# Two halves of the TensorE array for the products of a two-layer graph kernel

## The chip, the cores and the metric

The kernel runs on one core of a Trainium2 chip. The metric is device time in microseconds. Before the change it takes 2409.18 us, the median of three runs (2409.16 to 2414.54).

## The reference

There are 16 graphs (batches) of 1024 nodes with 128 features, each with a dense 1024 x 1024 adjacency matrix of zeros and ones. Two layers follow each other, each with a residual sum and a normalisation over the features:

```python
# layer 0
h = x @ Ww.T + Wb
e = (h @ A) @ h.T;  e = e + e.T
attention = softmax(where(adj > 0, e, 0), axis=1) * adj
hp = relu(attention @ h)
ic, fc, oc = three gates: sigmoid(hp @ wi_u + x @ wi_x), ...
x = layernorm(x + oc * tanh(ic * hp + fc * x))
# layer 1, with four heads
h = x @ conv_w[hd] + conv_b[hd]
scores = (h @ attn_w[hd]) @ h.T
hh = relu(tanh(adj * scores) @ h)
x = layernorm(x + relu(relu(mean of hh over the heads) + x))
```

Everything is in fp32. The largest parts of the work are, for each batch, the four 1024 x 1024 score matrices of layer 1 (a product over 128 features) and the four products of their tanh with h (a product over 1024 nodes).

## The kernel before

A product on TensorE has a stationary operand (128 rows by up to 128 columns, loaded into the array) and a moving operand, of which up to 512 columns stream past it; the result lands in a bank of PSUM, with the stationary columns as partitions. Everywhere in this kernel the contraction uses 128 rows, and in nearly all products the stationary operand has 128 columns.

Layer 1 is the larger part. For each batch there are 4 heads times 8 blocks of 128 nodes, 32 steps. `layer1_step` (line 687) of one step issues two score products (line 704), one for each half of 512 moving columns, into two PSUM tiles of the pool `ps_sc`, which has four of them. VectorE (DVE) multiplies each with the adjacency (line 705), ScalarE applies tanh to the 1024 columns (line 706), and `back` (line 708) multiplies the result with h of this block and head, accumulating over the 8 blocks into `acc`, two banks of PSUM (line 710). `back` isn't issued at once: `push` (line 194) holds it back for two steps. After a head's last block `add_head` (line 722) takes relu of the accumulator and adds it to a sum over heads; the next head reuses the same two banks.

Before the steps of a batch, `rows` (line 670) computes h of all four heads for each block (line 675), and `head_uT` with `project_T` (line 234, product in line 238) computes uT of a head, the operand of its scores.

Layer 0 of the next batches is woven into these steps. Its pieces have short names: Q is qT (`project_T`), H is h (`multiply_h`, line 335), S the scores (line 354), T their transposition through DVE and memory, A mask and exponentials, B the weighing with attention (`back` in line 455, product in line 462). The dictionaries `BETWEEN`, `AHEAD` and `FIRST` say after which step which piece is issued. This order is written by hand and each engine executes its own instructions in the order of the program; a framework inserts the waits between engines. Batch 0's layer 0 and the last head of the last batch have an order of their own, in which transpositions go through TensorE.

Of the kernel before, what the change touches and what calls it, by code (L numbers as in the profile page):

```python
# [19 lines left out]
P = 128  # L20
# [4 lines left out]
def two_layer_adjacency_kernel(  # L25
# [19 lines left out]
    nc = tc.nc  # L45
    B, N, D = x.shape
    H = conv_w.shape[0]
    assert D == P and N % 512 == 0
    NB = N // P
    NH = N // 512  # L50
# [10 lines left out]
    def small(name):  # L61
        return ps_sc.tile([P, 512], F32, tag="sc", name=name)
# [23 lines left out]
    wwT_g = consts.tile([P, G], F32, name="wwT_g")  # L86
# [39 lines left out]
    q_w = consts.tile([P, P], F32, name="q_w")  # L126
    c_col = wwT_g[:, G - 1 : G]
# [6 lines left out]
    def keep_at_work(n):  # L134
        for _ in range(n):
            nc.tensor.matmul(idle[:, :P], warm[:, :P], warm[:, :P], start=True, stop=True)  # L136

    keep_at_work(6)
    pa, pw, ps, pc = small("p_a"), small("p_ww"), small("p_s"), small("p_c")
    nc.tensor.transpose(pa[:, :P], a_in, ident)  # L140
# [53 lines left out]
    def push(back):  # L194
        pending.append(back)
        if len(pending) > DELAY:
            pending.popleft()()
# [33 lines left out]
                ALU.subtract, ALU.mult,  # L231
            )

    def project_T(dst, w, src, bias, name, halves=range(NH)):

        for q in halves:
            ps = small(f"pT_{name}_{q}")
            nc.tensor.matmul(ps, w, src[:, ts(q, 512)], start=True, stop=True)  # L238
            if bias is None:
                nc.scalar.copy(dst[:, ts(q, 512)], ps)  # L240
            else:
                nc.scalar.activation(dst[:, ts(q, 512)], ps, AF.Identity, bias=bias)
# [44 lines left out]
    def layer0(b):  # L287
# [3 lines left out]


        t = {}

        def load_xT():
            t["xT"] = sb.tile([P, N], F32, tag="xT", name=f"xT_{b}")
            nc.sync.dma_start(t["xT"], xT[b])
# [10 lines left out]
        def project_q(q):  # L308
            if q == 0:
                t["qT"] = sb.tile([P, N], F32, tag="qT0", name=f"qT0_{b}", bufs=1)  # L310
            if (b, q) == (0, 1):
                ps = small("pT_q0_second")
                nc.tensor.matmul(ps, q_w, t["xT"][:, 512:], start=True, stop=True)
                nc.vector.tensor_scalar_add(t["qT"][:, 512:], ps, c_col)
                return
            if (b, q) != (0, 0):
                return project_T(t["qT"], q_w, t["xT"], c_col, f"q0_{b}", [q])
            t["pq"] = small("pT_q0_first")
            nc.tensor.matmul(t["pq"], q_w, t["xT"][:, :512], start=True, stop=True)

# [6 lines left out]
        def multiply_h(g):  # L327

            if g == 0:
                t["h"] = sb.tile([P, NB, G], F32, tag="h0", name=f"h0_{b}", bufs=1)  # L330
            ks = GROUPS[g]
            ps = small(f"pR_h0_{b}_{g}")[:, : len(ks) * G]
            t["ph", g] = ps = ps.rearrange("p (k d) -> p k d", d=G)
            for i, k in enumerate(ks):
                nc.tensor.matmul(ps[:, i, :], t["xT"][:, ts(k, P)], wwT_g, start=True, stop=True)  # L335

        def add_h(g):
            h, ks = t["h"], GROUPS[g]
# [8 lines left out]
        def score(j, halves=None):  # L347
            if j == 0 and "R" not in t:

                t["R"] = sb.tile([P, NB, NB, P], F32, tag="R", name=f"R_{b}", bufs=1)  # L350
            for q in range(j // BH, NH) if halves is None else halves:
                ps = ps_sc.tile([P, 512], F32, tag="sc", name=f"sc0_{b}_{j}_{q}")
                lo, at = max(q * 512, j * P), (q + 1) * 512
                nc.tensor.matmul(  # L354
                    ps[:, : at - lo], t["qT"][:, ts(j, P)], t["xT"][:, lo:at], start=True, stop=True
                )
                to = t["R"][:, lo // P : at // P, j, :]
                psv = ps[:, : at - lo].rearrange("p (k d) -> p k d", d=P)
                r = t["h"][:, j, G - 1 : G]
                nc.scalar.activation(to, psv, AF.Identity, bias=r)  # L360
# [43 lines left out]
        def row(j):  # L404


            if (b, j) not in ((0, 0), (0, 1)):
                return t["R"][:, :, j, :]
            if ("row", j) not in t:
                w = sb.tile([P, N], F32, tag="turn", name=f"row_{j}", bufs=2)  # L410
                t["row", j] = w.rearrange("p (k d) -> p k d", d=P)
            return t["row", j]
# [42 lines left out]
        def back(j, halves=range(NH)):  # L455
            if j == 0:
                acc = ps_acc.tile([P, N], F32, tag="acc0", name=f"acc0_{b}")

                other = ps_acc.tile([P, N], F32, tag="acc1", name="acc_other") if b == 0 else acc
                t["acc"] = [acc[:, :512], other[:, 512:]]  # L460
            for q in halves:
                nc.tensor.matmul(  # L462
                    t["acc"][q], t["hz", j], row(j)[:, ts(q, BH), :],
                    start=(j == 0), stop=(j == NB - 1),
                )
# [158 lines left out]
        for g in range(len(GROUPS)):  # L624
            pieces[f"H{g}"] = partial(multiply_h, g)
            pieces[f"h{g}"] = partial(add_h, g)
# [5 lines left out]
        for q in range(NH):  # L632
            pieces[f"Q{q}"] = partial(project_q, q)
        for j in range(NB):
            for name, piece in (
                ("L", load_adj), ("E", find_edges), ("S", score), ("A", mask_exp), ("B", weigh)
            ):
                pieces[f"{name}{j}"] = partial(piece, j)
            if j + 1 < NB:
                pieces[f"T{j}"] = partial(turn_score, j)  # L640
# [29 lines left out]
    def rows(b, ks):  # L670

        for k in ks:
            h1_t[b, k] = sb.tile([P, H * D], F32, tag="h1", name=f"h1_{b}_{k}", bufs=NB + 1)
            ps = small(f"pR1_{b}_{k}")
            nc.tensor.matmul(  # L675
                ps, x1T_t[b][:, ts(k, P)], cw.rearrange("p h d -> p (h d)"), start=True, stop=True
            )
            nc.scalar.copy(h1_t[b, k], ps)  # L678

    def head_uT(b, hd, halves=range(NH)):  # L680
        if (b, hd) not in u_t:
            u_t[b, hd] = sb.tile([P, N], F32, tag="uT1", name=f"uT1_{b}_{hd}")
        project_T(u_t[b, hd], ms[:, hd, :], x1T_t[b], None, f"u1_{b}_{hd}", halves)
# [3 lines left out]
    def layer1_step(b, hd, m):  # L687
        x1T, h1, uT = x1T_t[b], h1_t[b, m], u_t[b, hd]
        adj = adj_t[b, m]
        if m == 0:  # L690
            acc1_t[b, hd] = ps_acc.tile([P, N], F32, tag="acc1", name=f"acc1_{b}_{hd}")
        acc = acc1_t[b, hd]


        last = (b, hd) == (B - 1, H - 1)
        if last:
            if m == 0:
                kept.append(sb.tile([P, NB, N], F32, tag="R", name="kept", bufs=1))
            s = kept[0][:, m, :]
        else:  # L700
            s = sb.tile([P, N], F32, tag="s1", name=f"s1_{b}_{hd}_{m}", bufs=4)
        for q in range(NH):
            ps = ps_sc.tile([P, 512], F32, tag="sc", name=f"sc1_{b}_{hd}_{m}_{q}")
            nc.tensor.matmul(ps, x1T[:, ts(m, P)], uT[:, ts(q, 512)], start=True, stop=True)  # L704
            nc.vector.tensor_mul(s[:, ts(q, 512)], ps, adj[:, ts(q, 512)])  # L705
        nc.scalar.activation(s, s, AF.Tanh)  # L706

        def back(halves=range(NH)):
            for q in halves:
                nc.tensor.matmul(  # L710
                    acc[:, ts(q, 512)], h1[:, ts(hd, D)], s[:, ts(q, 512)],
                    start=(m == 0), stop=(m == NB - 1),
                )
            if m == NB - 1:
                if hd == 0:
                    sum_t[b] = sb.tile([P, N], F32, tag="sum", name=f"sum_{b}", bufs=1)
                for q in halves:
                    add_head(b, hd, acc[:, ts(q, 512)], q * 512)

        push(partial(back, [0]) if last else back)  # L720

    def add_head(b, hd, a, at):

        o = sum_t[b][:, at : at + a.shape[1]]
        if hd == 0:
            nc.vector.tensor_scalar_max(o, a, 0.0)
        else:
            nc.vector.scalar_tensor_tensor(o, a, 0.0, o, op0=ALU.max, op1=ALU.add)  # L728
# [110 lines left out]
    run(second, "S4")  # L839
    head_uT(0, 0, [0])  # L840
    rows(0, range(0, BH - 1))
    turn_first_x1(x1_t[0], 1)
    rows(0, range(BH - 1, BH))
    head_uT(0, 0, [1])
    run(second, "T0 T1")
    land()
    run(second, "T2 E0")
    rows(0, range(BH, NB))
    land()

# [20 lines left out]
    for b in range(B):  # L871
        plan = BETWEEN if b else {**BETWEEN, **FIRST}
        after = layer0(b + 2) if b + 2 < B else {}
        for step in range(H * NB):
            hd, m = divmod(step, NB)
# [81 lines left out]
```

## Time and profile before

| What | Value |
|---|---|
| Median of the runs | 2409.18 us |
| Profiled execution: span from first to last instruction | 2407.4 us |
| TensorE, matmuls busy | 2398.8 us, 5983 records |
| TensorE, weight loads busy | 1095.6 us, 5983 records |
| DVE busy | 1551.3 us |
| ScalarE (ACT) busy | 1063.5 us |
| GpSimd (POOL) busy | 608.9 us |
| Mean granted TensorE clock | 0.999 |
| Score products of layer 1 (line 704) | 2048 records, 962.8 us |
| Products with h of layer 1 (line 710), all full steps | 2016 records, 947.3 us |

The profile is of one execution. Its time is known as its span, 2407.4 us; 1.8 us separate it from the median of the runs. "PE" is TensorE's matmuls, "PEld" its weight loads. In a group's line stand the line of the kernel, the engine, the operation, what is written and what is read, the shapes (rows * columns of the stationary operand, then the moving operand), the number of records, busy time and mean duration in ns, and the idle time just before. A matmul's end is modelled, and neighbouring records overlap, so the distance between starts says more than a duration. In the view in order of time, the columns are start and length of a merged stretch in us, the engine, the line and the records in it.

### The profile page before, as it was taken

The page shows a single profiled execution, that of the slowest core. Times are in us where ns is not written, and L with a number is a line of the kernel's source. Part 1 is how long each engine was busy: PE and PEld are TensorE (multiplying, and loading weights), DVE is VectorE, ACT ScalarE, POOL GpSimd, SP SyncE. Part 2 cuts the span into 40 slices and gives each one's busy share as a digit, 9 for nine tenths or more (in the row PEclk, how much of TensorE's full clock was granted, in tenths as well). Part 3 has the DMA queues.
Part 4 walks back from the last instruction along what each step waited for, and adds up shares of the span by engine and source line. Part 5 has one row for each costly group of instructions (what it writes and reads, how often), then busy time and mean ns, then how long its engine had stood idle before and what let it go on. Part 6 is the DMA issues. An engine that isn't in the chain of part 4 may idle for free.

```text
span 2407.4 us, 20166 instructions
## 1 busy us (share of the span) xinstructions
PE 2398.8 (100%) x5983; PEld 1095.6 (46%) x5983; DVE 1551.3 (64%) x3262; ACT 1063.5 (44%) x1503; POOL 608.9 (25%) x389
## 2 busy tenths in 40 slices
PE   9999999999999999999999999999999999999999
PEld 5444444444444444444444444444444444444444
DVE  7666666766667656666666666667666576666555
ACT  6545344453444534445444454444444344443333
POOL 2214131241312313133131231313214132141000
PEclk9999999999999999999999999999999999999999
DMA  5334151442414324243242422425234252341010
GB/s 192 72 78 123 46 130 42 97 106 50 126 47 104 94 60 115 53 111 82 63 113 62 115 69 70 110 56 123 62 78 108 51 131 53 80 115 34 18 27 10
DMA packets 474194, 196.98 MB, mean 82 GB/s; under 512 B 414948, under 2 KB 440291, under 8 KB 474084
## 3 DMA queue, kind: packets, MB, share of 16 engines
q1 hardware_dynamic: 455501, 129.03, 23.0%
q0 software_dynamic: 18288, 66.59, 9.3%
q8 instruction: 48, 0.79, 0.1%
q14 instruction: 63, 0.51, 0.1%
q10 hardware_dynamic: 294, 0.07, 0.0%
HBM read 136.12 MB, written 59.51 MB: 81 GB/s over the span
## 4 chain that ended last, share of the span: by engine, by line
PE 99%; DVE 1%; ACT 0%; issue 0%; POOLq 0%; DVEq 0%
PE sc L704 36%; PE acc L710 36%; PE acc L462 9%; PE sc L354 5%; PE pR L675 5%; PE pT_u L238 5%; PE pR_h L335 1%; PE pT_q L238 1%; PE acc_other L462 0%; PE idle L136 0%; DVE R L418 0%; DVE s L705 0%; PE pt L496 0%; DVE st L214 0%; PE turn L371 0%
## 5 line engine op out<-in xcount | busy, mean ns | idle before, releaser
L705 DVE TENSOR_TENSOR s<-sc,adj 128x512 f32<-128x512 f32 x1008 | 685.1, 688 | 713.9 <-PE sc L704 692.7
L706 ACT ACTIVATE s<-s 128x1024 f32<-128x1024 f32 x504 | 533.1, 1058 | 1056.9 <-DVE s L705 897.7
L704 PE MATMUL sc<-uT,x1T 128*128 128x512 f32 x2048 | 962.8, 592 | 0.2
L710 PE MATMUL acc<-s,h 128*128 128x512 f32 x2016 | 947.3, 592 | 0.0
L710 PEld LDWEIGHTS acc<-s,h 128*128 128x128 f32 x2016 | 380.5, 190 | 484.7 <-issue 476.7
L704 PEld LDWEIGHTS sc<-uT,x1T 128*128 128x128 f32 x2048 | 386.7, 190 | 470.2 <-issue 403.5
L401 POOL TENSOR_SCALAR edge<-adj 128x1024 uint8<-128x1024 f32 x120 | 332.8, 2773 | 315.3 <-DVE top_None L418 312.9
L218 POOL TENSOR_TENSOR rs<-rs,mhalf 128x8 f32<-128x8 f32 (+3 forms) x35 | 54.2, 1549 | 881.0 <-DVE rs L217 880.9
L462 PE MATMUL acc<-R,hz 128*128 128x512 f32 x492 | 231.6, 592 | 0.2 <-ACT hz L448 0.2
L430 ACT ACTIVATE R<-R,nmax 128x1024 f32<-128x1024 f32 x126 | 144.6, 1147 | 81.0 <-DVE nmax L426 73.3
L418 DVE CUSTOM_DVE_ANT_0 R<-R,edge 128x1024 f32<-128x1024 f32 x126 | 152.8, 1213 | 0.5 <-ACT hz L448 0.5
L451 DVE TENSOR_TENSOR R<-R,adj 128x1024 f32<-128x1024 f32 (+1 forms) x127 | 152.0, 1197 | 0.0
L462 PEld LDWEIGHTS acc<-R,hz 128*128 128x128 f32 x492 | 93.1, 190 | 115.7 <-issue 111.4
L354 PE MATMUL sc<-xT,qT 128*128 128x512 f32 (+3 forms) x384 | 144.9, 486 | 0.0
L360 ACT ACTIVATE R<-sc,h 128x512 f32<-128x512 f32 (+1 forms) x192 | 111.1, 580 | 52.3 <-PE sc L354 46.8
L543 POOL TENSOR_TENSOR x1T<-hp,wu_b 128x1024 f32<-128x1024 f32 x45 | 106.4, 2363 | 103.8 <-DVE hws L549 63.6
L238 PE MATMUL pT_u<-x1T,ms 128*128 128x512 f32 x256 | 120.6, 593 | 0.0
L675 PE MATMUL pR<-cw,x1T 128*128 128x512 f32 x256 | 117.6, 598 | 0.0
L354 PEld LDWEIGHTS sc<-xT,qT 128*128 128x128 f32 x384 | 69.9, 190 | 70.0 <-issue 60.6
L302 POOL DMA_DIRECT2D adj<-in_adjT_dram x112 | 66.1, 590 | 91.8 <-DVE s L705 91.8
L728 DVE SCALAR_TENSOR_TENSOR sum<-acc,sum 128x512 f32<-128x512 f32 x95 | 61.2, 686 | 41.7 <-PE acc L710 41.7
L678 ACT COPY h<-pR 128x512 f32<-128x512 f32 x128 | 72.4, 593 | 28.2 <-PE pR L675 26.4
(163 smaller groups left out, 1151.5 us busy)
## 6 DMA issues: line engine op xcount, KB each, us to landing
adj<-in_adjT_dram POOLq DMA_DIRECT2D x112, 512.0 KB, 4.1
xT<-in_xT_dram SPq DMA_DIRECT2D x16, 512.0 KB, 4.7
adj<-in_adjT_dram SPq DMA_DIRECT2D x16, 512.0 KB, 8.8
x<-in_x_dram SPq DMA_DIRECT2D x16, 512.0 KB, 5.5
dram_hp<-turn_hp SPq DMA_DIRECT2D x15, 512.0 KB, 2.6
hp<-dram_hp SPq DMA_DIRECT2D x60, 128.0 KB, 3.1
dram_x<-turn_x SPq DMA_DIRECT2D x15, 512.0 KB, 2.9
x1T<-dram_x SPq DMA_DIRECT2D x60, 128.0 KB, 5.5
```

What stands on the lines that cost most here:

```text
L238: nc.tensor.matmul(ps, w, src[:, ts(q, 512)], start=True, stop=True)
L354: nc.tensor.matmul(ps[:, : at - lo], t["qT"][:, ts(j, P)], t["xT"][:, lo:at], start=True, stop=True)
L401: engine.tensor_scalar(m, adj_t[b, j], 0.0, None, ALU.is_gt)
L418: nc.vector.tensor_tensor_reduce(to[:, ks], s[:, ks], t["edge", j][:, ks], 1.0, nmax, ALU.mult, ALU.max, top)
L430: nc.scalar.activation(row(j), row(j), AF.Exp, bias=t["nmax", j], accum_out=t["z", j])
L451: nc.vector.tensor_mul(s[:, ks], s[:, ks], adj[:, ks])
L462: nc.tensor.matmul(t["acc"][q], t["hz", j], row(j)[:, ts(q, BH), :], start=(j == 0), stop=(j == NB - 1),)
L675: nc.tensor.matmul(ps, x1T_t[b][:, ts(k, P)], cw.rearrange("p h d -> p (h d)"), start=True, stop=True)
L704: nc.tensor.matmul(ps, x1T[:, ts(m, P)], uT[:, ts(q, 512)], start=True, stop=True)
L705: nc.vector.tensor_mul(s[:, ts(q, 512)], ps, adj[:, ts(q, 512)])
L706: nc.scalar.activation(s, s, AF.Tanh)
L710: nc.tensor.matmul(acc[:, ts(q, 512)], h1[:, ts(hd, D)], s[:, ts(q, 512)], start=(m == 0), stop=(m == NB - 1),)
```

## The change

A new helper `halves_mm` issues a product as two: stationary columns 0 to 63 with the output on partitions 0 to 63, then columns 64 to 127 with partitions 64 to 127, both with the same moving operand. It replaces the single matmul in layer 1's scores, h and uT for all batches, and in layer 0's products (qT, h, scores, weighing) for all batches but the first. For the products with h of layer 1, `back` issues eight half products in a step where it issued two products: each has 64 stationary columns and 256 moving columns, neighbouring ones go to different halves of the array and different halves of the 1024 columns, and so to different banks of the accumulator. Only the first block's first pieces in a bank carry the start flag. The last head's steps, which handle one half of the columns, use `halves_mm`. Transposes, the set-up of the weights and the tail products (line 750) stay as they were.

```diff
+    def halves_mm(out, lhsT, rhs, start, stop):
+        for c in range(2):
+            nc.tensor.matmul(out[ts(c, 64)], lhsT[:, ts(c, 64)], rhs, start=start, stop=stop)
...
-    def project_T(dst, w, src, bias, name, halves=range(NH)):
+    def project_T(dst, w, src, bias, name, halves=range(NH), split=True):
...
-            nc.tensor.matmul(ps, w, src[:, ts(q, 512)], start=True, stop=True)
+            (halves_mm if split else nc.tensor.matmul)(
+                ps, w, src[:, ts(q, 512)], start=True, stop=True
+            )
...
+        mm = halves_mm if b else nc.tensor.matmul
...
-                nc.tensor.matmul(ps[:, i, :], t["xT"][:, ts(k, P)], wwT_g, start=True, stop=True)
+                mm(ps[:, i, :], t["xT"][:, ts(k, P)], wwT_g, start=True, stop=True)
...
-                nc.tensor.matmul(
+                mm(
                     ps[:, : at - lo], t["qT"][:, ts(j, P)], t["xT"][:, lo:at], start=True, stop=True
                 )
...
-                nc.tensor.matmul(
+                mm(
                     t["acc"][q], t["hz", j], row(j)[:, ts(q, BH), :],
                     start=(j == 0), stop=(j == NB - 1),
                 )
...
-            nc.tensor.matmul(
+            halves_mm(
                 ps, x1T_t[b][:, ts(k, P)], cw.rearrange("p h d -> p (h d)"), start=True, stop=True
             )
...
-            nc.tensor.matmul(ps, x1T[:, ts(m, P)], uT[:, ts(q, 512)], start=True, stop=True)
+            halves_mm(ps, x1T[:, ts(m, P)], uT[:, ts(q, 512)], start=True, stop=True)
...
         def back(halves=range(NH)):
-            for q in halves:
-                nc.tensor.matmul(
-                    acc[:, ts(q, 512)], h1[:, ts(hd, D)], s[:, ts(q, 512)],
-                    start=(m == 0), stop=(m == NB - 1),
-                )
+            if len(halves) < NH:
+                for q in halves:
+                    halves_mm(
+                        acc[:, ts(q, 512)], h1[:, ts(hd, D)], s[:, ts(q, 512)],
+                        start=(m == 0), stop=(m == NB - 1),
+                    )
+            else:
+                for d in range(2):
+                    for r in range(2):
+                        for c in range(NH):
+                            q = (c + d) % NH
+                            at = slice(q * 512 + r * 256, q * 512 + r * 256 + 256)
+                            nc.tensor.matmul(
+                                acc[ts(c, 64), at], h1[:, hd * D + c * 64 : hd * D + c * 64 + 64],
+                                s[:, at], start=(m == 0 and r == 0), stop=(m == NB - 1),
+                                skip_group_check=True,
+                            )
```

More of the change, by code (lines that the diff above doesn't have):

```diff
@@ L316, in project_q @@
             if (b, q) != (0, 0):
-                return project_T(t["qT"], q_w, t["xT"], c_col, f"q0_{b}", [q])
+                return project_T(t["qT"], q_w, t["xT"], c_col, f"q0_{b}", [q], split=b > 0)
             t["pq"] = small("pT_q0_first")
```

## The prediction

> **What bounds the kernel now.** I read the page first: the busy line of each engine, the row of granted clocks, and the chain that ended last.
>
> ```profile
> span 2407.4 us, 20166 instructions
> ...
> PE 2398.8 (100%) x5983; PEld 1095.6 (46%) x5983; DVE 1551.3 (64%) x3262; ACT 1063.5 (44%) x1503; POOL 608.9 (25%) x389
> ...
> PEclk9999999999999999999999999999999999999999
> ...
> PE 99%; DVE 1%; ACT 0%; issue 0%; POOLq 0%; DVEq 0%
> ```
>
> TensorE is busy for the whole span, at a mean clock of 0.999 (the view by core), and is 99% of the chain. "Busy" alone doesn't say that it works at its peak, so I then took the groups of TensorE with shapes kept apart, and its order of time.
>
> ```profile
> L704 PE MATMUL sc<-uT,x1T 128*128 128x512 f32 x2048 | 962.8, 592 | 0.2
> L710 PE MATMUL acc<-s,h 128*128 128x512 f32 x2016 | 947.3, 592 | 0.0
> ...
> L335 PE MATMUL pR_h<-wwT_g,xT 128*128 128x132 f32 x256 | 32.2, 276 | 0.3 <-DVE sb_col L162 0.3
> ...
> L354 PE MATMUL sc<-xT,qT 128*128 128x256 f32 x64 | 19.0, 379 | 0.0
> L354 PE MATMUL sc<-xT,qT 128*128 128x128 f32 x64 | 12.3, 274 | 0.0
> ```
>
> ```profile
> 1000.47 1.88 PE L704 MATMUL sc<-uT,x1T 128*128 128x512 f32 x4
> 1002.18 1.88 PE L710 MATMUL acc<-s,h 128*128 128x512 f32 x4
> 1003.90 1.88 PE L462 MATMUL acc<-R,hz 128*128 128x512 f32 x4
> ```
>
> Three readings. One product is two records (1024 score products, x2048), which I call passes. The mean durations rise by (592 - 379) / 256 = 0.83 ns per moving column, so 512 columns stream for 426 ns; the remaining 166 ns of a record is latency that overlaps the next one. Four passes start every 1.72 us, 430 ns each; read to the nanosecond, starts lie 429 to 430 ns apart, 2.5 ns over the stream. 128 columns stand at 109 to 112. All 5983 passes, at two array cycles per column, come to 2374 us of pure streaming, out of 2401 us from the first start to the last end. The 27 us between are about 15 us of these 2.5 ns and 12 us of longer gaps, 9 of them in the first 100 us. Nothing waits: the waits of TensorE add up to 2.7 us, all near the start or the end.
>
> Weight loads are hidden under the previous pass:
>
> ```profile
> 1000.04 0.19 PEld L704 LDWEIGHTS sc<-uT,x1T 128*128 128x128 f32 x1 [0.24 <-issue]
> 1000.47 0.19 PEld L704 LDWEIGHTS sc<-uT,x1T 128*128 128x128 f32 x1 [0.24 <-issue]
> ```
>
> Each load starts as the pass before its own starts (1 to 3 ns after, in nearly all cases). Loads that come closest stand 108 ns apart, so 128 columns of weights take that long and 64 some 54 (estimate: half).
>
> **What the Trainium skill says.** "FP8 and Floating Point Precision", section TensorE Precision Notes: true fp32 is four passes through the array. The trace agrees: two records, each at two cycles per column (0.83 ns at the 2.4 GHz of the TensorE page). "TensorEngine Tiling (Array Packing)", Key Properties: tiles work independently, weight loads and matmuls of different tiles can run in parallel, and a change of mode drains the engine. "TensorE: Matmul & The Clock Gate", Part 3, The mechanism: matmuls start in program order, tiles about 4 ns apart, and weight loads can be pulled ahead where they don't conflict. No run here shows two halves at work: every row of the trace but a 3-row one has 128*128.
>
> **The change, part by part.** A half product has 64 stationary columns and still streams all moving columns twice. If both halves overlap, the array does the same four passes, so the price of a product can't fall below two pass times. Program order on TensorE (H is the high pass, L the low one) is H0 L0 H1 L1 for halves 0 and 1, then the next product. L0 has to follow H0 on its half (429 ns), H1 may run beside L0, L1 beside the next H0. A product still costs two slots, 858 ns, plus two hand-overs from half to half.
>
> Counts after the change: 1024 score pairs of layer 1, 128 of its h, 128 for uT, 30 for qT, 180 scores and 240 weighings and 120 h of layer 0 (batches 1 to 15), 8 for the last head: 1858 pairs of half products. The 504 full steps of the product with h have 8 half products of 256 columns: 2016 pairs.
>
> Sum, on the profiled 2407.4 us (1.8 under the median of 2409.2, which I add at the end):
> 1. 256 columns in place of 512: a step has, on each half, 8 passes of 215.8 ns (the start-to-start after 256 columns) where it had 4 of 429.2: 1726 - 1717 = 9.6 ns, times 504: +4.8 us.
> 2. Hand-overs: 2 x (1858 + 2016) = 7748. Bounds: 0 (the load is ready, the start coincides) and the skill's 4 ns, which is 31 us. Each has hundreds of ns of queued work ahead of it, so I take 1 ns: +7.7 us.
> 3. Mode changes: 16 in the whole program order (13 while batch 0 of layer 0 still uses the full width, 3 in the tail). A drain is the 166 ns of latency; on half of them one half stands idle for a pass, 429 ns: 16 x 0.166 + 8 x 0.43 = +6 us. Bounds 0 and twice that.
> 4. A wait that has no slack. At the change of heads the two DVE additions (line 728, or 726) free the accumulator for the next head:
>
> ```profile
> 1149.23 1.88 PE L704 MATMUL sc<-uT,x1T 128*128 128x512 f32 x4
> 1149.43 1.29 DVE L726 TENSOR_SCALAR sum<-acc 128x512 f32<-128x512 f32 x2 [1.02 <-PE acc L710]
> ...
> 1150.84 0.30 PEld L710 LDWEIGHTS acc<-s,h 128*128 128x128 f32 x2 [0.55 <-issue]
> 1150.95 0.59 PE L710 MATMUL acc<-s,h 128*128 128x512 f32 x1
> ```
>
> DVE is done at 1150.72, the load starts at 1150.84 and the pass at 1150.95, with no gap before it. Some 30 loads (two in each batch) sit like this, 316 ns after the preceding pass began. After the change the last pass on half 1 ends one 256-column slot (216 ns) later against the stream, and the load is 54 ns shorter: about 0.16 us of stall, 30 times: +4.8 us. Behind this load, in order, is everything on TensorE; DVE and ScalarE are covered by their own slack. Bounds 0 and 30 x 0.43 = 13.
> 5. Longer latency of a product (one pass, 0.43 us, until DVE may read): hidden. DVE sits idle 714 us before its 1008 multiplications of line 705, and tanh is used two steps (over 6.8 us) later. Without this cover it would cost 0.43 us in each of 512 steps.
> 6. Twice to four times the instructions: a load and a pass every 108 ns on average in the 256-column stretches. The trace issues such pairs every 109 to 112 ns at 128 columns, limited there by the stream itself, so I price it at 0; the memory traffic of the data and all DMA queues are untouched.
>
> 2407.4 + 4.8 + 7.7 + 6 + 4.8 = 2430.7, and with the 1.8 us around it about 2433 us (+1.0%). With the bounds of 2 to 4 this case runs from 2414 to 2470.
>
> **Rivals.** (a) *Weight loads are exposed.* If the queue is strictly in order, the load for H1 can't start before L0 has started (in the trace no load starts ahead of the previous pass, though on one half there was no room for it anyway). Then each hand-over costs a load of 64 columns, 54 ns: 7748 x 54 = 418 us, in place of the 7.7: about 2840 us. For it: the in-order starts; against it: the skill's pulled-ahead loads. (b) *The halves don't overlap*, say because both compete for one stream of moving data that a pass of fp32 already fills. Then every steady pass is paid twice. About 2330 of the 2399 busy us are steady: about 4750 us. Against it: the skill's independent tiles. (c) *Faster.* The fixed 2.5 ns per pass could vanish behind the other half. There are 2 x 1858 + 2016 = 5732 old passes of this kind, 14.3 us, and item 1 goes with it: 2395 us if also 2 to 4 cost nothing. It decides from the point where the savings exceed the losses by 7 us; items 3 and 4 alone eat 11 of the 14, which speaks against it. A rate under two cycles per column would gain far more, but four passes leave no room for it. (d) *No change to be measured*: halves overlap and 2 to 4 come to under 2 us, 2414.
>
> **How the numbers follow.** Overlap with small losses: 0.45. Rival (d): 0.14. Rival (a): 0.17. Rival (b): 0.13. Rival (c): 0.11. A measurement of this kernel can't tell less than about 0.3%, 7 us, from no change. Slower: 0.45 + 0.17 + 0.13 = 0.75; same 0.14; faster 0.11. The range takes in the first case, (c) down to its price, (d), and (a): 2395 to 2850; it leaves out (b) and a rate that nothing here shows.
>
> **What would show it.** In the changed trace: records with 64 columns, and starts of the low pass of half 0 and the high pass of half 1 within a few ns (overlap), 54 ns apart and more (a), or a whole pass apart (b). Slots of 429 and 216 ns confirm items 1 and 2. A gap on TensorE before the first product with h of a head, 30 times, is item 4. A clock below 0.99, DVE multiplications that end tens of us of TensorE's waits, or passes that take longer when both halves stream would make the prediction wrong.

## The result and the profile after

| | before | after |
|---|---|---|
| Median | 2409.37 us (2409.02 to 2414.66) | 2415.60 us (2414.57 to 2421.16) |
| Runs | 17 | 17 |
| Ratio, with its 95% interval | | 1.0026 [1.0019, 1.0033] |

The change costs 6.2 us, 0.26%. The forecast was 2433, +24 us. The profiled execution of the changed kernel took 2420.8 us, for a span of 2419.0. In this one execution the array ran at half clock until 17.4 us from the start (passes of 512 columns stood 853 ns apart, and 429 later), and until 5.0 us in the profile of before, which puts it some 5 us behind, so what follows uses the medians, and the profile from 40 us on.

The page of the changed kernel, the busy line, the row of granted clocks and the chain that ended last:

```profile
span 2419.0 us, 39731 instructions
...
PE 2410.0 (100%) x15747; PEld 1141.4 (47%) x15747; DVE 1551.6 (64%) x3262; ACT 1063.7 (44%) x1503; POOL 609.1 (25%) x389
...
PEclk9999999999999999999999999999999999999999
...
PE 98%; DVE 1%; DMA 0%; issue 0%; SPq 0%; ACT 0%; POOL 0%; POOLq 0%; DVEq 0%
```

TensorE has 2.6 times as many records and is still 98% of the chain; the other engines are as busy as before. The groups of TensorE, shapes kept apart (line 140 is the helper `halves_mm`, line 728 the product with h):

```profile
L140 PE MATMUL sc<-uT,x1T 128*64 128x512 f32 x4096 | 966.5, 592 | 0.2
L728 PE MATMUL acc<-s,h 128*64 128x256 f32 x8064 | 956.3, 379 | 0.4 <-DVE sum L747 0.4
```

Twice the records of 512 columns, at the same 592 ns each, fill the same time: 966.5 us where 2048 records filled 962.8. Busy time is the union of the records here, so the halves work at the same time. The product with h rises from 947.3 to 956.3 us, with four times the records. Its records last 379 ns, exactly what 256 columns took at full width before. The order of time shows the same for one step, and below it are the weight loads of its first records:

```profile
999.78 1.89 PE L140 MATMUL sc<-uT,x1T 128*64 128x512 f32 x8
1001.50 1.90 PE L728 MATMUL acc<-s,h 128*64 128x256 f32 x16
1003.22 1.89 PE L140 MATMUL acc<-R,hz 128*64 128x512 f32 x8
```

```profile
1000.21 0.14 PEld L140 LDWEIGHTS sc<-uT,x1T 128*64 128x64 f32 x2 [0.28 <-DVE nmax L433]
1000.64 0.14 PEld L140 LDWEIGHTS sc<-uT,x1T 128*64 128x64 f32 x2 [0.28 <-issue]
```

Eight score records take 1.72 us from start to start, as four did. Loads come in pairs, one for each half, 0.43 us apart, all under the running passes. Read to the nanosecond, every slot holds two passes, whose starts lie 6 to 8 ns apart (36 ns in a few stretches); the slots are 429 to 430 ns long at 512 columns and 215.8 at 256, as at full width.

Which half a record belongs to isn't in the trace, but the beginning of a stretch tells it. When the array changes from full width to halves, 96 ns pass without a stream, so nothing of before is left in it and the first pass is the high one of half 0, which the program issues first. If the order of the program (high and low pass of half 0, then of half 1) were kept over both halves, it would run alone for a slot. The starts are these, in ns from the first one, from the trace at 52.10 us:

```
score product of layer 0, 512 columns     0    7   480   ...
```

The second pass starts 7 ns after the first and 473 ns before the third. The low pass of half 0 can't start before the high one has streamed (429 ns), so the second is the high pass of half 1. Each half is fed by itself: both high passes, then both low ones.

### The profile page after: what moved, and what is told of

The parts are those of the page before. It is cut to its first block, busy times and chain, and to the rows that moved or that the text cites. A ratio compares the mean times of both kernels' runs of the same rounds, so it can differ in the third digit from the quotient of the medians.

```text
span 2419.0 us, 39731 instructions
## 1 busy us (share of the span) xinstructions
PE 2410.0 (100%) x15747; PEld 1141.4 (47%) x15747; DVE 1551.6 (64%) x3262; ACT 1063.7 (44%) x1503; POOL 609.1 (25%) x389
## 4 chain that ended last, share of the span: by engine, by line
PE 98%; DVE 1%; DMA 0%; issue 0%; SPq 0%; ACT 0%; POOL 0%; POOLq 0%; DVEq 0%
PE sc L140 41%; PE acc L728 36%; PE acc L140 9%; PE pT_u L140 5%; PE pR L140 5%; PE pR_h L140 1%; PE pT_q L140 1%; PE sc L361 0%; PE acc L469 0%; PE acc_other L469 0%; DVE s L712 0%; DVE st L218 0%; PE idle L136 0%; DMA dram_turn<-turn 0%; DMA R<-dram_turn 0%
## 5 line engine op out<-in xcount | busy, mean ns | idle before, releaser
L140 PE MATMUL sc<-uT,x1T 128*64 128x512 f32 x4096 | 966.5, 592 | 0.2
L728 PE MATMUL acc<-s,h 128*64 128x256 f32 x8064 | 956.3, 379 | 0.4 <-DVE sum L747 0.4
L728 PEld LDWEIGHTS acc<-s,h 128*64 128x64 f32 x8064 | 580.3, 137 | 505.6 <-issue 273.8
L140 PEld LDWEIGHTS sc<-uT,x1T 128*64 128x64 f32 x4096 | 294.3, 137 | 472.6 <-issue 359.3
L140 PE MATMUL acc<-R,hz 128*64 128x512 f32 x960 | 226.4, 592 | 0.0
L140 PE MATMUL sc<-xT,qT 128*64 128x512 f32 (+2 forms) x720 | 136.5, 486 | 0.0
L140 PE MATMUL pT_u<-x1T,ms 128*64 128x512 f32 x512 | 121.0, 592 | 0.0
L140 PE MATMUL pR<-cw,x1T 128*64 128x512 f32 x512 | 117.3, 595 | 0.0
L140 PEld LDWEIGHTS acc<-R,hz 128*64 128x64 f32 x960 | 68.9, 137 | 91.7 <-issue 76.5
L246 ACT COPY uT<-pT_u 128x512 f32<-128x512 f32 x128 | 71.4, 580 | 20.0 <-PE pT_u L140 20.0
```

The source lines that it names most:

```text
L140: nc.tensor.matmul(out[ts(c, 64)], lhsT[:, ts(c, 64)], rhs, start=start, stop=stop)
L728: nc.tensor.matmul(acc[ts(c, 64), at], h1[:, hd * D + c * 64 : hd * D + c * 64 + 64], s[:, at], start=(m == 0 and r == 0), stop=(m == NB - 1),
```

## The experiments

None of the variants changes what is computed; two of them compute one product twice. The kernel before ran beside all of them, at 2409.39 (33 runs), 2409.36 (3) and 2409.49 us (11).

**What 256 columns cost.** The first variant gives `back` 512 moving columns again, other ones on each half, so a step has four half products.

```diff
-                    for r in range(2):
+                    for r in range(1):
...
-                            at = slice(q * 512 + r * 256, q * 512 + r * 256 + 256)
+                            at = slice(q * 512, q * 512 + 512)
```

> The changed kernel with 512 moving columns in its products with h of layer 1, still other ones on each half (four half products in a step instead of eight). Theory A, the halves run side by side and only the fixed 2.5 ns of each extra 256-column pass and the mode changes cost time: 504 steps x 9.6 ns = 4.8 us come back, less some 0.5 us by which the wait at the change of batch grows again; about 2411 us, 1.5 to 2 us over the kernel before. Theory B, each hand-over from half to half costs about 0.8 ns (6.2 us over 7748 of them): 2016 fewer hand-overs, 1.6 us back, about 2414 us. Theory C, the cost sits in the start and the tail alone: no change, 2415.6 us.

Measured: 2410.33 us (13 runs, 2409.5 to 2416.8), ratio to before 0.9997 [0.9989, 1.0006]. That is 5.3 us less than the changed kernel, and within the measurement of before. Nearly the whole cost of the change lies in the 256 columns.

The second variant is the reverse: the kernel before, at full width, whose product with h is cut into pieces of 256 columns.

```diff
+            w = 512 if len(halves) < NH else 256
...
-                nc.tensor.matmul(
-                    acc[:, ts(q, 512)], h1[:, ts(hd, D)], s[:, ts(q, 512)],
-                    start=(m == 0), stop=(m == NB - 1),
-                )
+                for r in range(512 // w):
+                    at = slice(q * 512 + r * w, q * 512 + r * w + w)
+                    nc.tensor.matmul(
+                        acc[:, at], h1[:, ts(hd, D)], s[:, at],
+                        start=(m == 0 and r == 0), stop=(m == NB - 1), skip_group_check=True,
+                    )
```

> The kernel before, at full width everywhere, with 256 moving columns in the products with h of layer 1 (four products in a step instead of two). Theory A: the same 9.6 ns in each of 504 steps without any halves: +4.0 to +4.8 us, about 2413.5 to 2414.2 us. Theory B and C: nothing but the hand-overs or the start costs, 2409.4 us.

Measured: 2414.41 us (13 runs, 2413.95 to 2419.63), ratio 1.0017 [1.0009, 1.0025], 5.0 us over before; 504 steps times 9.6 ns are 4.8. The cost has nothing to do with the halves. In the order of time of this variant eight full-width records take the 1.73 us that the sixteen take in the changed kernel:

```profile
1001.23 1.89 PE L713 MATMUL acc<-s,h 128*128 128x256 f32 x8
1002.96 1.45 PE L704 MATMUL sc<-uT,x1T 128*128 128x512 f32 x3
```

**What the mode changes cost.** The third variant adds to the first one that every product ahead of layer 1's first step is at full width, so the array changes its mode 4 times, not 16.

```diff
+    steady = []
...
     def halves_mm(out, lhsT, rhs, start, stop):
+        if not steady:
+            return nc.tensor.matmul(out, lhsT, rhs, start=start, stop=stop)
...
+    steady.append(True)
```

> As the kernel with 512 columns on other halves, and every product before the first step of layer 1 at full width, so that the mode changes fall from 16 to 4. Theory A: in the trace each change costs about 0.095 us and the first pass after it 0.04 to 0.1 us more; 12 fewer are 1.3 to 2 us less, about 2409.6 us, level with the kernel before. Theory B: no change against the kernel with 512 columns, or with all of its cost in hand-overs still some 4 us over the kernel before.

Measured: 2409.43 us (13 runs, 2409.08 to 2414.36), ratio 0.9993 [0.9985, 1.0001]. The median is 0.9 us under the first variant's and level with before. The intervals overlap, so the 0.9 alone is an indication, not more. The profiles show the same directly. From the second product of batch 0's weighing that reads `R` (`acc<-R,hz`) to the first score product of layer 1, this variant takes 31.74 us; the changed kernel and the five variants with the same work there take 32.49 to 32.51. That is 0.76 us for 12 changes, 64 ns each. For 30 changes of heads, the hand-overs of all products and nearly twice as many records together, the interval of this variant leaves at most 0.3 us over the kernel before.

**Whether the halves overlap, and who waits for whom.** Two variants issue layer 1's products for h again with the same result, once for half 0 alone and once for both halves. This is the one where only half 0 repeats; for the other, the condition never holds.

```diff
-            halves_mm(
-                ps, x1T_t[b][:, ts(k, P)], cw.rearrange("p h d -> p (h d)"), start=True, stop=True
-            )
+            for _ in range(2):
+                for c in range(2):
+                    if _ and c and True:
+                        continue
+                    nc.tensor.matmul(
+                        ps[ts(c, 64)], x1T_t[b][:, ts(2 * k + c, 64)],
+                        cw.rearrange("p h d -> p (h d)"), start=True, stop=True,
+                    )
```

> The changed kernel with the half product on half 0 issued a second time (the same values written again) in the 128 products of h of layer 1. Half 0 has 2 x 429 ns more in each: 128 x 0.858 = 110 us more, about 2525 us, with overlap and without.

> The same with the half products on both halves issued a second time. Theory A, the second half's extra work runs beside the first's: the same 110 us, about 2525 us. If the halves took turns: 220 us, about 2635 us.

Measured: 2523.18 us (2 runs) for half 0 alone, 2522.69 us (2 runs) for both; ratios 1.0465 [1.0433, 1.0497] and 1.0463 [1.0431, 1.0495]. That is 107.6 and 107.1 us over the changed kernel, for 128 products of 0.858 us = 109.8. The second half's repetition is free beside the first's. In the trace, half 0 alone first, then both:

```profile
63.94 6.97 PE L686 MATMUL pR<-cw,x1T 128*64 128x512 f32 x22
70.33 0.64 PE L140 MATMUL sc<-uT,x1T 128*64 128x512 f32 x1
```

```profile
63.85 7.04 PE L686 MATMUL pR<-cw,x1T 128*64 128x512 f32 x32
70.72 1.46 PE L140 MATMUL sc<-uT,x1T 128*64 128x512 f32 x6
```

From start to start, 22 records in 6.39 us against 32 in 6.87: the latter are 16 slots of 429 ns with two passes in each. Work on one half is hidden by equal work on the other, and uneven work is paid for by the longer half. A kernel whose halves didn't overlap would have paid 220 us for the repetition of both.

**Whether weight loads are shared.** With pieces of 64 columns a pass streams for 53.3 ns and needs a load of 54 (the estimate of the prediction; behind a mode change the load for the low pass starts 54 to 55 ns after that for the high one).

```diff
-                    for r in range(2):
+                    for r in range(512 // 64):
...
-                            at = slice(q * 512 + r * 256, q * 512 + r * 256 + 256)
+                            at = slice(q * 512 + r * 64, q * 512 + r * 64 + 64)
```

> The changed kernel with 64 moving columns in the products with h of layer 1: 32 half products in a step, 32 passes on each half. If weight loads of the two halves run side by side as well, a pass costs 64 columns x 0.83 + 2.5 = 56 ns (a load of 64 columns takes about 54): 1.79 us in a step, +0.065 us over the changed kernel, 504 times, about +33 us, 2448 us. If both halves share one port for weights, two loads of 54 ns stand behind each pair of passes, 108 ns: 3.46 us in a step, +1.73 us, 504 times, +870 us, about 3290 us. If the issue of instructions binds at a pair of load and pass in 27 ns or more, it lies between.

Measured: 2485.89 us (2 runs), ratio 1.031 [1.0279, 1.0342], 70.3 us over the changed kernel. The order of time shows a step:

```profile
1000.02 2.06 PE L728 MATMUL acc<-s,h 128*64 128x64 f32 x64
1001.88 1.92 PE L140 MATMUL acc<-R,hz 128*64 128x512 f32 x8
```

64 records in 1.86 us are 32 pairs at 58 ns, and 32 x 58.3 - 1726 = 140 ns for each of 504 steps are the 70 us. If loads of the two halves took turns, a pair would take two loads, 108 ns. They run side by side, and a load and a pass are issued every 29 ns. The 58 ns are 5 over the stream, not the 2.5 that each pass had so far. The same edit with 128 columns tells whether that is the number of passes:

```diff
-                    for r in range(2):
+                    for r in range(512 // 128):
...
-                            at = slice(q * 512 + r * 256, q * 512 + r * 256 + 256)
+                            at = slice(q * 512 + r * 128, q * 512 + r * 128 + 128)
```

> The changed kernel with 128 moving columns in the products with h of layer 1, 16 passes on each half in a step. Theory A with a fixed 2.5 ns per pass: 8 passes more than with 256 columns, 20 ns in a step, 504 times, +10 us, about 2425.7 us. If weight loads (54 ns each, two per 109 ns slot) already bind: more than that, up to the 4.7 ns per pass that remain over the stream at 64 columns, +19 us, 2435 us.

Measured: 2426.04 us (4 runs, 2424.71 to 2426.32), ratio 1.0065 [1.005, 1.008]: 10.4 us over the changed kernel, and 8 more slots x 2.5 ns x 504 = 10.1. The fixed 2.5 ns of a pass stand at 512, 256 and 128 columns alike, and only at 64 is there more. Full width shows the same where a load is as long as the stream: in the tail of the kernel before, products of 128 columns (line 750) start 111 to 112 ns apart, 5 over their stream of 106.7, while transpositions (line 740), whose records of loads are shorter (140 ns against 192), start 109 apart. So a load as long as the stream is the likely reason; no run tested it.

**How far ahead the other half is fed.** The order of the half products in `back` is changed: all four of half 0 (eight passes), then all of half 1.

```diff
-                for d in range(2):
-                    for r in range(2):
-                        for c in range(NH):
+                for c in range(NH):
+                    for d in range(2):
+                        for r in range(2):
```

> The changed kernel with the eight half products of a step in another order: four on half 0, then four on half 1. Theory A with a queue of its own for each half that looks far ahead: half 1 starts on its four while half 0 works, as before, 2415.6 us. If the queue looks ahead by one product only (the two records of it): in each step half 1 starts three products of 2 x 216 ns late and half 0 then idles as long at the next hand-over, up to 1.3 us in each of 504 steps, up to 650 us more.

Measured: 2519.54 us (2 runs), ratio 1.045 [1.0418, 1.0481], 104 us over the changed kernel, 206 ns in each step. In its order of time neighbouring groups now overlap, since the halves are shifted against each other:

```profile
1003.34 0.60 PE L728 MATMUL acc<-s,h 128*64 128x256 f32 x2
1003.72 0.59 PE L140 MATMUL sc<-uT,x1T 128*64 128x512 f32 x1
1003.77 1.73 PE L728 MATMUL acc<-s,h 128*64 128x256 f32 x11
1005.13 0.64 PE L140 MATMUL acc<-R,hz 128*64 128x512 f32 x1
```

Half 0 starts its eight passes at 1003.34, 1003.55 and so on. The last score pass of half 1 starts at 1003.72, so this half is free at 1004.14; its first load of the step starts at 1004.205, right after half 0's fifth pass started (1004.200), and takes some 54 ns, uncovered: half 1 stands for 0.11 us. Then half 0 waits for its next load in the same way, until the fifth pass of half 1. So half 1's work is taken up only when three passes of half 0 are still to start; with eight in turn that is late. With two half products of each in turn (four passes) it should be soon enough:

```diff
-                    for r in range(2):
-                        for c in range(NH):
+                    for c in range(NH):
+                        for r in range(2):
```

> The changed kernel with the half products of a step in the order two on half 0, two on half 1, and again. With four on each in turn, the first load of half 1 was issued when the fifth of the eight passes of half 0 began, with three of them still to start. If the queue can hold three passes of one half while it feeds the other, two half products (four passes) in turn just fit: level with the changed kernel, 2415.6 us, at most a few us more. If each run of more than one half product on the same half costs a late load of some 55 ns at both ends: four changes of half in a step, 504 steps, about 110 us more, as with four in turn.

Measured: 2416.3 us (8 runs, 2415.46 to 2421.92), ratio 1.0034 [1.0023, 1.0044], 0.7 us from the changed kernel, level with it. Four passes in turn cost nothing that can be told, eight cost 206 ns. The limit was not narrowed further, nor was it tried whether it counts passes, loads or instructions.

None of these beats the kernel before; the first and the third are level with it.

## Why the prediction was right or wrong

The sum of the prediction was 23.3 us of losses; 6.2 were measured. Its direction was right and the halves overlap, but the likeliest case didn't come true; the outcome is rival (d), 2414 us. Of the measured 6.2 us, 5.3 are the 256 columns. The other 0.9 is 1.2 us of mode changes, less 0.6 that the halves win back at the changes of batch (item 3), and 0.3 that the runs don't resolve.

**Item 1 (256 columns, 4.8 us) was right**: 5.3 between the changed kernel and its 512-column variant, 5.0 at full width.

**Item 2 (7748 hand-overs at 1 ns, 7.7 us) is the step that failed**, with the order behind it: "H0 L0 H1 L1 for halves 0 and 1 ... two slots, 858 ns, plus two hand-overs from half to half". There is no hand-over. A half starts its next pass when its own last pass has streamed, not when the other half has started something, so a slot lasts 429 to 430 ns as before and the term is 0. The section on the kernel before says that each engine executes its instructions in the order of the program; over the two halves of TensorE that doesn't hold. I had taken the program order from the Trainium skill, "TensorE: Matmul & The Clock Gate", Part 3, The mechanism; these traces fit it within a half and contradict it across the two. The 6 to 8 ns between the starts of a pair are an offset that stays, not a delay that adds up: where it is 36 ns, or 58 as in the variant with two half products in turn, the slots are as long. The skill's "TensorEngine Tiling (Array Packing)", Key Properties, that tiles work independently, is what holds here.

**Item 3 (16 mode changes, 6 us) was too large**: 1.2 us for all 16. The size of one drain, 166 ns, was about right where it lies; that "on half of them one half stands idle for a pass" (3.4 of the 6 us) was wrong, since the halves end 7 ns apart; and more than half of what the changes do cost where they lie doesn't reach the end. The order of time of layer 0's first batch shows a change, before and after:

```profile
36.97 1.12 PE L462 MATMUL acc<-R,hz 128*128 128x512 f32 x2 [0.23 <-ACT hz L448]
37.94 1.02 PE L462 MATMUL acc_other<-R,hz 128*128 128x512 f32 x2
38.80 0.84 PE L335 MATMUL pR_h<-wwT_g,xT 128*128 128x132 f32 x6
39.47 1.88 PE L462 MATMUL acc<-R,hz 128*128 128x512 f32 x4
```

```profile
42.64 1.13 PE L469 MATMUL acc<-R,hz 128*128 128x512 f32 x2
43.60 1.02 PE L469 MATMUL acc_other<-R,hz 128*128 128x512 f32 x2
44.56 0.90 PE L140 MATMUL pR_h<-wwT_g,xT 128*64 128x132 f32 x12
45.38 1.98 PE L469 MATMUL acc<-R,hz 128*128 128x512 f32 x4
```

From start to start, the two full passes ahead of the halves take 0.96 us in place of 0.86, the twelve small passes 0.82 in place of 0.67, and the four full passes behind them (until 47.20, before until 41.19) 1.82 in place of 1.72: 0.35 us for two changes. To the nanosecond, 15 of the 16 changes leave 95 to 97 ns between the end of the stream and the next start (the other leaves 153), and the first pass behind a change carries its own weight load uncovered: 51 ns to halves, and to full width 105, or 55 to 59 for three transpositions. All 16 come to some 2.7 us so. What reaches layer 1 is the distance of these lines, before and after:

```profile
31.28 1.02 PE L462 MATMUL acc<-R,hz 128*128 128x512 f32 x2
...
62.92 3.60 PE L704 MATMUL sc<-uT,x1T 128*128 128x512 f32 x8
```

```profile
36.75 1.02 PE L469 MATMUL acc<-R,hz 128*128 128x512 f32 x2
...
69.25 3.60 PE L140 MATMUL sc<-uT,x1T 128*64 128x512 f32 x16
```

It is 32.50 us in place of 31.64, for 13 changes. From the first product with h of the last head (`acc<-kept,h`) to the end of TensorE's work it is 24.52 in place of 24.17, for three. Together that is 1.2 us. One reason why the rest is swallowed is in the first line of the first view under this item: a wait of 0.23 us for `hz` of ScalarE. The third variant, at full width there, has this wait too; the variant with 128 columns, which has the mode changes and comes to this point at nearly the same time, hasn't:

```profile
37.34 1.12 PE L473 MATMUL acc<-R,hz 128*128 128x512 f32 x2 [0.23 <-ACT hz L459]
```

```profile
37.52 1.12 PE L469 MATMUL acc<-R,hz 128*128 128x512 f32 x2
```

The prediction hadn't asked what slack there was in front of the changes. Nor had it a term for what halves gain: at each change of batch a pass of layer 1's h waits for its load, before and after, and on halves 51 ns of the next load are uncovered where it was 105. A batch takes 148.72 us in the third variant and 148.77 before, and the stretch between the start and the last head 2314.2 in place of 2314.8, 0.6 us less.

**Item 4 (change of heads, 4.8 us) didn't happen.** The same stretch of the changed kernel:

```profile
1157.42 1.89 PE L140 MATMUL sc<-uT,x1T 128*64 128x512 f32 x8
1157.63 1.29 DVE L745 TENSOR_SCALAR sum<-acc 128x512 f32<-128x512 f32 x2 [1.03 <-PE acc L728]
...
1159.04 1.53 PEld L728 LDWEIGHTS acc<-s,h 128*64 128x64 f32 x16 [0.62 <-issue]
1159.13 1.68 PE L728 MATMUL acc<-s,h 128*64 128x256 f32 x14
```

From the score products to the products with h it is 1.71 us, and before it was 1.72. The stall was expected because half 1 would end a slot later than the old product; both halves end together, so nothing is later. The loads of the two halves, 54 ns shorter as I had said, start 94 and 65 ns before their passes, where the old one started 113 before. The wait has hardly any slack, as before, and costs nothing, as before. One stall is new, in the list of TensorE's waits:

```profile
PE acc L728 <- DVE sum L747: 0.4, 1, 0.4
```

It occurs once, at a change of heads, for a DVE addition behind a late transfer. It isn't alone: the lists of five of the nine variants have the same wait, once each, of 0.3 to 1.3 us (1.3 in the first variant), and those of the kernel before and of the second and third variants don't. With one profile of each, whether the change brings it stays open; it may be in the 0.3 us that the runs don't resolve.

**Item 5** (the longer latency of a product) was put at nothing because tanh comes two steps later. It is nothing without that cover: a half product ends when the old product did. **Item 6** (instructions) was right; pairs at 29 ns in the 64-column variant show how far it is from a limit.

**The rivals.** (a), exposed weight loads at 2840 us, fell by the order of time: loads stand in pairs under running passes. It is not absurd, though: with eight passes in turn the loads are exposed. (b), no overlap at 4750 us, fell by the repetition of both halves, which costs what the repetition of one does. (c), a gain of the 2.5 ns per pass, fell: they stay on each half, at 512, 256 and 128 columns. (d) was given 0.14. The prediction's own numbers come to about 2417 us, close to it, if item 2 is taken at its lower bound, with the reason that it gave itself (each hand-over has hundreds of ns of work queued), and if item 4 and the idle half of item 3, which stand on the same order, follow it. One assumption carried 16 of the 23 us, so these terms moved together.

## What to carry to other kernels

In this fp32 kernel, two halves of 64 columns do the work of a full-width product in the same time, with no gain and no loss, as long as both always have work in reach: alternate them product by product, or by four passes (eight cost 206 ns a step, and nothing between was tried), and keep their work equal. What costs is short streams, 2.5 ns for every pass, at full width too, and a mode change, 0.17 us where it lies, of which less than half reached the end here. When several terms of a sum rest on one picture of the machine, ask what the sum becomes without it.

## What the runs showed that was not expected

- The passes of the two halves mostly start within 6 to 8 ns, and a half doesn't wait for the other's place in the program's order: the high pass of half 1 starts more than 400 ns ahead of the low pass of half 0.
- This reaches a limited way ahead. With eight passes in turn the other half's load starts at the fifth, and a step loses 206 ns; with four, nothing.
- Weight loads of the two halves run side by side: 58 ns for a pair of passes, each with a load of some 54 ns.
- A change of mode leaves 95 to 97 ns between the streams, and then the first load is uncovered, 51 ns for halves and 105 ns for full width.
